# Four attention layers on one core: three output projections transposed, keys in chunks of 121, transposes of four heads in three banks, order by searched ranks

## The chip, the core and the metric

The kernel runs on one core of one Trainium2 chip. The time is device microseconds of one execution, and of several executions the median counts.

## What is computed

For each of 16 batches, `x` (100 queries by 256) passes through four cross-attention layers against one context (361 keys by 256), all in float32 with 16 heads. Each layer adds its output to a residual. L0 and L3 have heads of 16 columns, L1 and L2 of 64.

```
L0: q = LN(x) wq + bq; k, v = LN(ctx) wk + bk, wv + bv      # 16 heads of 16
    x = x + softmax(q k^T / 4) v wo + bo
    x = x + gelu(LN(x) w1 + b1) w2 + b2                      # 256 -> 1024 -> 256
L1: q = RMS(x) wq; k, v = ctx wk, ctx wv                     # 16 heads of 64
    x = x + softmax(q k^T) v wo                              # 1024 -> 256
L2: q, k = rope(x Wq), rope(ctx Wk); v = ctx Wv              # 16 heads of 64
    x = LN(x + softmax(mask(q k^T / 8)) v Wo) * gamma + beta # 1024 -> 256
L3: as L0's attention, with its own weights and norms
```

## The kernel before

**A plan, then an order.** Nothing is emitted while the layers are described. `plan.add` (L119) records each piece of work: the engines that may do it with an occupancy and a latency in ns, what it reads and writes, which buffer it takes, and for TensorE the tile shape (`mode`): `row64` and `row32` put several groups of contracted rows side by side, `col64` and `col32` several groups of output columns. `order` (L159) then walks through a list schedule: of the works whose inputs and buffers are at hand it takes the one that can start first, and among equals the one of lowest rank, `batch * 3e4 - tail`, where the tail is the longest chain behind it. A change of tile shape costs `MODE_SWITCH`, and 100 ns more if the present shape has run for under 1500 ns (L205 to L207). Copies out of PSUM may go to ACT or to VectorE, whichever the plan has ready first (`copied`, L542). The instructions are emitted in that order (L1206), and each engine runs its own in it.

**Batches.** Two batches are in flight: even ones use the buffers of parity 0, odd ones those of parity 1. SP loads context, x and mask two batches ahead; all 12 weight slabs stay in SBUF.

**Banks.** PSUM is a pool of 8 banks `ps` for everything; at most 4 hold scores.

**A unit of attention** (L726) is four heads. Their scores go into four banks, 100 queries by 361 keys each (L740). Per head: in L2 a minimum against the mask (L787), the negated row maximum on VectorE (L790), the exponential with its sum on ACT (L793); per pair of heads the reciprocal (L765); per head the division on POOL (L772). Then `transposed` (L805), once per pair: 12 transposes in `row64`, the two halves of the queries (64 and 36) into two banks, and two copies into a `pT` buffer, of which there are four, for two heads each. A chunk of keys is 128 columns (128, 128, 105), the last one padded with zeros. `weighted` (L835) multiplies by the values, accumulating over the three chunks, into one bank (L851), and copies it to `oT`, which holds the heads' outputs transposed: 128 columns of the concatenated heads by 100 queries, in two chunks (L0, L3) or eight.

**Projections.** Queries, keys and the hidden layer come out transposed (`project_T`, L632): weights stationary, activations moving. The output projection (`project_out`, L887) does it the other way round: a chunk of `oT` is stationary (100 columns), the weights move (256 columns), the result has the queries as rows, and VectorE adds the residual (L900). All these matmuls are issued at one line, L627 in `on_columns`. Where a layer needs its input transposed, `queries_T` (L593) makes it: four transposes and two copies. Norms are taken over rows of queries (`inv_root`, L553). `keys_T` (L643) transposes the context twice per batch, raw and normed, 12 transposes and three copies each. `add_row` (L877) adds a bias row to the residual on POOL.

Of the kernel before, what the change touches and what calls it, by code (L numbers as in the profile page):

```python
# [22 lines left out]
KC = (128, 128, SK - 256)  # L23
SKP = NKC * P
# [28 lines left out]

class Buf:
# [12 lines left out]
class Work:  # L67
    __slots__ = (
        "engines", "fn", "bufs", "takes", "next", "then", "n_after", "ready", "tail", "batch",
        "mode", "modes", "index", "start", "end", "engine",  # L70
# [4 lines left out]
HOP = 60  # L75
# [20 lines left out]
class Plan:  # L96

    MODE_SWITCH = {"row64": 160, "row32": 175, "col64": 145, "col32": 130, None: 190}

    KEEP_MODE, RUN = 100.0, 1500.0  # L100
# [4 lines left out]
    def __init__(self, slots):  # L105
        self.free = {c: [(0.0, i) for i in range(len(t))] for c, t in slots.items()}
        self.slots = slots
        self.work = []
        self.queue = {}
        self.turn = {}  # L110
        self.batch = 0

# [6 lines left out]
    def add(self, engines, fn, reads=(), writes=(), takes=(), mode=None, begun=()):  # L119
# [35 lines left out]
        w.ready = 0.0  # L155
        self.work.append(w)
        return w

    def order(self, lag):  # L159
# [4 lines left out]
        free_at = {e: 0.0 for e in ("PE", "ACT", "DVE", "POOL", "SP", "DMA")}  # L164
        mode, run = None, 0.0
        ready = [w for w in self.work if not w.n_after]
        left = len(self.work)
        turn = {c: 0 for c in self.queue}
        done = []
        while left:  # L170
            ready.sort(key=lambda w: w.batch * lag - w.tail)
            best = None
            held = set()
            for w in ready:
                t = w.ready
                ok = True
                need = {}
                for b in w.takes:
                    need[b.cls] = need.get(b.cls, 0) + 1
                for c, k in need.items():  # L180
                    if c in held:
                        ok = False
                        break
                    if c in self.queue:
                        mine = [b for b in w.takes if b.cls == c]
                        q = self.queue[c]
                        if q[turn[c] : turn[c] + k] != mine:
                            ok = False
                            break
                    slots = self.free[c]  # L190
                    if len(slots) < k:
                        ok = False
                        held.add(c)
                        break
                    t = max(t, sorted(slots)[k - 1][0])
                if not ok:
                    continue
                engine, cost = None, None
                for e, occ, lat in w.engines:
                    s = max(t, free_at[e])  # L200
                    if e == "PE" and mode not in w.modes:
                        lat = lat + self.MODE_SWITCH[w.modes[0]]
                    if cost is None or s + lat < cost - 1:
                        engine, cost, start = e, s + lat, s
                late = start  # L205
                if engine == "PE" and mode not in w.modes and run < self.RUN:
                    late += self.KEEP_MODE  # L207
                if best is None or late < best[0] - 1e-6:
                    best = (late, w, engine, cost, start)
            assert best is not None, [(w.index, [b.name for b in w.takes]) for w in ready[:20]]  # L210
            _, w, e, end, start = best
            occ = next(o for n, o, _ in w.engines if n == e)
            if e == "PE":
                run = run + occ if mode in w.modes else occ
                if mode not in w.modes:
                    mode = w.modes[0]
                    occ += self.MODE_SWITCH[mode]
                w.mode = mode
            free_at[e] = start + occ
            w.start, w.end, w.engine = start, end, e  # L220
            if e != "PE":
                w.mode = e
            for b in w.takes:
                slots = self.free[b.cls]
                slots.sort()
                _, i = slots.pop(0)
                b.slot, b.ap = i, self.slots[b.cls][i]
                if b.cls in turn:
                    turn[b.cls] += 1
            for b in w.bufs:  # L230
                b.left -= 1
                b.at = max(b.at, end + HOP)
                if not b.left and b.cls:
                    self.free[b.cls].append((b.at, b.slot))
            for x in w.next:
                x.n_after -= 1
                x.ready = max(x.ready, end + (0 if len(x.engines) == 1 and x.engines[0][0] == e else HOP))
                if not x.n_after:
                    ready.append(x)
            for x in w.then:  # L240
                x.n_after -= 1
                x.ready = max(x.ready, start)
                if not x.n_after:
                    ready.append(x)
            ready.remove(w)
            done.append(w)
            left -= 1
# [4 lines left out]
def tile_xattn_layers(  # L252
# [18 lines left out]
    def slots_of(name, n, shape, dtype=F32, pool=const):  # L271
# [8 lines left out]
        "pT": slots_of("pT", 4, [P, 2, NKC, S]),  # L280
# [11 lines left out]
    for p in range(2):  # L292
# [7 lines left out]
        slots[f"x{p}"] = slots_of(f"x{p}", 4, [S, E])  # L300
        slots[f"z{p}"] = slots_of(f"z{p}", 1, [S, E])
        slots[f"xT{p}"] = slots_of(f"xT{p}", 1, [P, 2, S])

# [5 lines left out]
    for t in slots["prob"]:  # L309
        nc.gpsimd.memset(t[:S, SK:], 0.0)  # L310
    for p in range(2):
# [13 lines left out]
    def load_inputs(b, issued=200.0, lands=4000.0):  # L325
# [3 lines left out]
        def issue(_):  # L329
            nc.sync.dma_start(  # L330
                out=ct.ap[:, 0:2, :], in_=ctx_kv[b, 0:256, :].rearrange("(c p) d -> p c d", p=P)
            )
            nc.sync.dma_start(out=ct.ap[: KC[2], 2, :], in_=ctx_kv[b, 256:SK, :])
# [219 lines left out]
    def inv_root(srcs, eps, name, square=False):  # L553
# [16 lines left out]
        def power(_):  # L570
# [5 lines left out]
            on_dve(350, k), stats, reads=[b for b, _, _ in srcs], writes=[mv]  # L576
# [16 lines left out]
    def queries_T(src, p, name):  # L593


        t = plan.buf(f"xT{p}", name)
# [7 lines left out]
        def fn(_):  # L604
# [7 lines left out]
            on_pe((64, 2), least=55), fn, reads=[src], writes=banks, takes=[t], mode="row64"  # L612
        )
        for i, (q0, q1) in enumerate(parts):
            copied(
                lambda q0=q0, q1=q1: t.ap[:, :, q0:q1], lambda i=i: tp(i), 2 * (q1 - q0),
                [banks[i]], [t],
            )
# [22 lines left out]
    HALVES = ((0, 64), (64, P))  # L641

    def keys_T(ct, cls, b):  # L643
# [4 lines left out]
        def tp(i):  # L648
            return banks[i].ap[:, : 2 * NKC * 64].rearrange("p (c j s) -> p c j s", c=2, j=NKC)

        def fn(_):
            for j, n in enumerate(KC):
                for c in range(2):
                    for i, (r0, r1) in enumerate(HALVES):
                        r1 = min(r1, n)
                        nc.tensor.transpose(
                            tp(i)[:, c, j, : r1 - r0], ct.ap[r0:r1, j, c * P : (c + 1) * P],
# [4 lines left out]
            on_pe((64, 2 * NKC), least=55), fn, reads=[ct], writes=banks, takes=[t], mode="row64"  # L662
        )

        def dst(i, j0, j1):
            a = t.ap[:, :, j0 * P : j1 * P].rearrange("p c (j s) -> p c j s", s=P)
            return a[:, :, :, 64 * i : 64 * i + 64]

        last = KC[2] - 64
        copied(lambda: dst(0, 0, NKC), lambda: tp(0), 2 * NKC * 64, [banks[0]], [t])  # L670
        copied(lambda: dst(1, 0, 2), lambda: tp(1)[:, :, 0:2, :], 4 * 64, [banks[1]], [t])
        copied(
            lambda: t.ap[:, :, 2 * P + 64 : SK], lambda: tp(1)[:, :, 2, :last], 2 * last,
            [banks[1]], [t],
        )
# [32 lines left out]
    class Attention:  # L708
# [17 lines left out]
        def unit(self, i):  # L726
# [27 lines left out]
            pTs = {}  # L754
            for u, pair in enumerate(pairs):
                pTs |= self.transposed([probs[h] for h in pair], pair, f"{name}_{i}_{u}")
# [48 lines left out]
        def transposed(self, probs, heads, name):  # L805

            banks = [plan.buf("ps", f"{name}_tp{t}") for t in range(2)]
            pT = plan.buf("pT", f"{name}_pT")
            parts = ((0, 64), (64, S))

            def tp(t):
                n = parts[t][1] - parts[t][0]
                return banks[t].ap[:, : 2 * NKC * n].rearrange("p (h c s) -> p h c s", h=2, c=NKC)

            def fn(_):
                for j, prob in enumerate(probs):
                    for c in range(NKC):
                        for t, (q0, q1) in enumerate(parts):
                            nc.tensor.transpose(  # L819
                                tp(t)[:, j, c, :], prob.ap[q0:q1, c * P : (c + 1) * P],  # L820
                                ident[q0:q1, q0:q1],
                            )

            plan.add(
                on_pe((64, 6), least=55), fn, reads=[*probs, self.v_buf(heads[0])], writes=banks,
                takes=[pT], mode="row64",
            )
            for t, (q0, q1) in enumerate(parts):
                copied(
                    lambda q0=q0, q1=q1: pT.ap[:, :, :, q0:q1], lambda t=t: tp(t),  # L830
                    2 * NKC * (q1 - q0), [banks[t]], [pT],
                )
            return {h: (pT, j) for j, h in enumerate(heads)}
# [74 lines left out]


    def small_heads_layer(L, b, xt, zT, names, fq, fk):  # L910
# [59 lines left out]
        for j, n in enumerate(KC):  # L970
            ps = plan.buf("ps", f"L{L}_v_ps_{b}_{j}")

            def values(mode, j=j, n=n, ps=ps):
                for c in range(2):
                    on_columns(
                        mode, lambda t0, t1: ps.ap[t0:t1, :E], zT.ap[:, c, j * P : j * P + n],
# [33 lines left out]
    def large_heads_layer(L, b, xt, xT, cT, names, rot, cap):  # L1010
# [48 lines left out]
        def values(half):  # L1059
            v = vb[half] = plan.buf(f"v{p}", f"L{L}_v_{b}_{half}")  # L1060
            for j, n in enumerate(KC):
                ps = plan.buf("ps", f"L{L}_v_ps_{b}_{half}_{j}")

                def fn(mode, j=j, n=n, ps=ps):
                    for c in range(2):
                        on_columns(
                            mode, lambda t0, t1: ps.ap[t0:t1, :], cT.ap[:, c, j * P : j * P + n],
# [28 lines left out]
        return project_out(att.oT, 8, wo, xt, p, f"L{L}_x_{b}")  # L1096

    def feed_forward(b, xt):
# [5 lines left out]
        resid = add_row(xt, f"ff_xb_{b}", "L0_xattn_b2", p, [rows_b])  # L1104
# [154 lines left out]
```

## Time and profile before

| | |
|---|---|
| median of 3 runs | 2068.08 us (2065.17 to 2068.21) |
| the profiled execution | 2067.87 us, its span 2066.0 us |
| TensorE clock granted | 0.988 of full speed over the span |
| instructions | 71,693, of which 29,665 matmul records and as many weight loads |
| costliest TensorE lines | L627 (all projections), L740 (scores), L851 (weighted sums), L819 (transposes of probabilities) |
| division on POOL (L772) | 1024 of 582 ns |
| exponential on ACT (L793) | 1024 of 567 ns, and 208 ns each to read the sum |
| maximum on VectorE (L790) | 1024 of 524 ns |
| copies to pT | 438 groups on ACT of 456 ns, 586 on VectorE of 418 ns |
| residual added on VectorE (L900) | 80 of 423 ns |
| from HBM / to HBM | 21.92 MB / 1.64 MB |

A float32 matmul leaves two matmul records, a transpose one. PE is TensorE's matmul side, PEld its weight loads, which overlap. A row of groups reads: line, engine, operation, what it writes and reads, rows*columns of the weights, moving operand, count, busy us, mean ns. A row of the timeline reads: start, length, group; the length of a group of matmuls runs to the end of its last one, which overlaps the next group, so costs are read from start to start. In brackets stands how long the engine was idle before it and what ended that.

### The profile page before, as it was taken

To read this page: it belongs to the slowest core of one execution; us is meant where nothing else is said; L and a number is where in the kernel's file an instruction comes from. 1 tells how busy PE (TensorE), PEld (TensorE's weight loads), DVE (VectorE), ACT (ScalarE), POOL (GpSimd) and SP (SyncE) were. 2 spreads that over 40 slices of the span, in tenths; PEclk is the share of its full clock that TensorE was granted. 3 is DMA by queue.
4 is the path that set the end of the run, shared out by engine and by line. 5 is a ranking of instruction groups with operands and counts; after the bars stand their busy time and mean duration, and the time that the engine had idled before them with its cause. 6 is when DMAs were issued, how large, how long until landed. Compare 5 with 4: busy or idle time off the path is not lost.

```text
span 2066.0 us, 71693 instructions
## 1 busy us (share of the span) xinstructions
PE 1993.2 (96%) x29665; PEld 1294.4 (63%) x29665; DVE 1375.9 (67%) x4058; ACT 1075.6 (52%) x3277; POOL 965.4 (47%) x1523
## 2 busy tenths in 40 slices
PE   8999999999999999999999999999999999999996
PEld 5666566575665656666575665756656566675664
DVE  5465666766677666766767667676776757667664
ACT  3445545555555455555555455554555545555453
POOL 4253545445354443644535354453545526455352
PEclk9999999999999999999999999999999999999996
DMA  7000000000000000000000000000000000000000
GB/s 285 2 2 12 4 10 4 4 12 5 12 5 3 11 5 12 5 11 4 5 12 4 12 3 4 12 4 12 5 2 12 4 12 4 10 5 4 2 4 3
DMA packets 14476, 28.13 MB, mean 14 GB/s; under 512 B 3346, under 2 KB 12360, under 8 KB 12616
## 3 DMA queue, kind: packets, MB, share of 16 engines
q1 hardware_dynamic: 14152, 23.56, 3.5%
q8 instruction: 233, 3.82, 0.8%
q14 instruction: 91, 0.75, 0.1%
HBM read 21.92 MB, written 1.64 MB: 11 GB/s over the span
## 4 chain that ended last, share of the span: by engine, by line
PE 85%; DVE 6%; POOL 4%; ACT 3%; issue 2%; DMA 0%; SPq 0%; DVEq 0%; ACTq 0%; POOLq 0%
PE ps L627 53%; PE ps L740 12%; PE ps L851 11%; PE ps L819 8%; ACT pT L547 3%; DVE two L790 1%; POOL prob L772 1%; POOL mv L571 1%; DVE ps L787 1%; DVE mv L561 1%; DVE ctxr L1145 1%; POOL kT L701 1%; PE ps L607 1%; PE ps L445 1%; DVE sw L689 1%
## 5 line engine op out<-in xcount | busy, mean ns | idle before, releaser
L772 POOL TENSOR_SCALAR prob<-prob,two 100x361 f32<-100x361 f32 x1024 | 578.2, 582 | 701.0 <-DVE two L765 544.4
L793 ACT ACTIVATE prob<-ps,two 100x361 f32<-100x361 f32 x1024 | 564.6, 567 | 149.2 <-DVE two L790 129.6
L790 DVE TENSOR_REDUCE two<-ps 100x1 f32<-100x361 f32 x1024 | 477.2, 524 | 193.3 <-PE ps L740 193.2
L627 PE MATMUL ps<-slab,cT 128*32 128x512 f32 (+3 forms) x2232 | 364.9, 596 | 3.7 <-ACT pT L547 3.7
L627 PE MATMUL ps<-cT,slab 128*64 128x361 f32 (+1 forms) x2360 | 351.0, 472 | 13.2 <-DVE kT L696 6.6
L547 ACT COPY pT<-ps 128x384 f32<-128x384 f32 (+1 forms) x438 | 185.7, 456 | 308.1 <-PE ps L819 220.1
L740 PE MATMUL ps<-kT,qT 32*100 32x181 f32 (+3 forms) x4096 | 301.5, 329 | 0.5 <-DVE qT L963 0.5
L819 PEld LDWEIGHTS ps<-ident,prob 64*128 64x128 f32 (+1 forms) x6144 | 227.4, 140 | 105.8 <-issue 58.7
L549 DVE COPY pT<-ps 128x216 f32<-128x216 f32 (+1 forms) x586 | 230.4, 418 | 93.4 <-PE ps L819 88.0
L740 PEld LDWEIGHTS ps<-kT,qT 32*100 32x100 f32 (+1 forms) x4096 | 227.5, 164 | 95.9 <-issue 39.9
L819 PE MATMUL ps<-ident,prob 64*128 64x64 f32 (+1 forms) x6144 | 261.9, 229 | 10.4 <-POOL prob L772 8.1
L627 PEld LDWEIGHTS ps<-cT,slab 128*64 128x64 f32 (+1 forms) x2360 | 132.6, 129 | 130.9 <-issue 95.4
L793 ACT ACTIVATION_READ_ACCUMULATOR prob<-ps,two 100x1 f32 x1024 | 212.6, 208 | 0.0
L627 PEld LDWEIGHTS ps<-slab,cT 128*32 128x32 f32 (+3 forms) x2232 | 94.8, 117 | 144.9 <-issue 134.1
L547 ACT COPY v<-ps 128x512 f32<-128x512 f32 (+1 forms) x151 | 88.7, 587 | 174.0 <-PE ps L627 174.0
L693 POOL TENSOR_TENSOR sw<-sw,rot 128x361 f32<-128x361 f32 x128 | 104.9, 822 | 157.0 <-DVE sw L689 148.1
L627 PE MATMUL ps<-xT,slab 128*64 128x100 f32 (+1 forms) x4576 | 172.6, 251 | 1.8 <-issue 1.4
L627 PEld LDWEIGHTS ps<-xT,slab 128*64 128x64 f32 (+1 forms) x4576 | 162.1, 126 | 19.3 <-issue 11.3
L851 PE MATMUL ps<-pT,v 128*64 128x100 f32 (+1 forms) x3072 | 157.1, 252 | 9.4 <-ACT pT L547 9.4
L851 PEld LDWEIGHTS ps<-pT,v 128*64 128x64 f32 (+1 forms) x3072 | 140.9, 137 | 35.1 <-issue 16.7
L627 PE MATMUL ps<-slab,oT 128*32 128x256 f32 (+2 forms) x1528 | 153.6, 386 | 0.0
L765 DVE RECIPROCAL two<-two 100x2 f32<-100x2 f32 x512 | 81.6, 160 | 91.3 <-ACT prob L793 86.2
(86 smaller groups left out, 1981.5 us busy)
## 6 DMA issues: line engine op xcount, KB each, us to landing
slab<-slabs_dram SPq DMA_DIRECT2D x12, 1024.0 KB
ctxr<-ctx_dram SPq DMA_DIRECT2D x16, 256.0 KB
ctxr<-ctx_dram SPq DMA_DIRECT2D x16, 105.0 KB
x<-x_dram SPq DMA_DIRECT2D x16, 100.0 KB
out_dram<-x SPq DMA_DIRECT2D x16, 100.0 KB
mask<-mask_dram SPq DMA_DIRECT2D x16, 45.1 KB
rows<-rowvecs_dram SPq DMA_DIRECT2D x1, 640.0 KB
cst<-consts_dram SPq DMA_DIRECT2D x1, 362.0 KB
```

Source lines behind the costliest of these rows:

```text
L445: nc.tensor.matmul(ps.ap[:, n : n + 1], lhsT=w[name][:, c, m * P : (m + 1) * P], rhs=col(b, c), start=(c == 0), stop=(c == 1),)
L547: nc.scalar.copy(dst(), src())
L549: nc.vector.tensor_copy(dst(), src())
L627: nc.tensor.matmul(out_f(t, t1), lhsT=lhsT[:, t:t1], rhs=rhs, start=start, stop=stop, tile_position=(0, t),)
L693: nc.gpsimd.tensor_tensor(a, a, wide(sin()), ALU.mult)
L740: nc.tensor.matmul(banks[h].ap[:S, k0:k1], lhsT=self.q_of(h), rhs=self.k_of(h)[:, k0:k1], start=(k0 == 0), stop=(k1 == SK), skip_group_che ...
L765: nc.vector.reciprocal(rsum.ap[:S], sums.ap[:S])
L772: nc.gpsimd.tensor_scalar(p.ap[:S, :SK], p.ap[:S, :SK], rsum.ap[:S, j : j + 1], 1.0, ALU.mult, ALU.mult,)
L790: nc.vector.tensor_reduce(neg_max.ap[:S, 0:1], s(), AX.X, ALU.max, negate=True)
L793: nc.scalar.activation(prob.ap[:S, :SK], s(), AF.Exp, bias=neg_max.ap[:S, 0:1], accum_out=sums.ap[:S, j : j + 1],)
L819: nc.tensor.transpose(tp(t)[:, j, c, :], prob.ap[q0:q1, c * P : (c + 1) * P], ident[q0:q1, q0:q1],)
L851: nc.tensor.matmul(ps.ap[t * w0 : (t + 1) * w0, cols], lhsT=lhsT, rhs=pTs[h][0].ap[:n, pTs[h][1], c, :], start=(c == 0), stop=(c == NKC - ...
```

## The change

1. **Projections transposed.** The output projections of the feed-forward, L1 and L2 use a new `project_out_T`: weights stationary (128 columns at a time, in column tiles of 64 or 32), `oT` moving (100 columns), the result transposed in a new buffer `rT` (two per parity), to which VectorE adds a residual that is transposed too. L0's and L3's keep the old form. After the feed-forward's `add_row` the residual is transposed once (`queries_T`, class `rT`). A new `rows_of` turns `rT` back into rows where a norm needs them: after the feed-forward and after L2. L2 takes L1's `rT` as its transposed input, and its own `queries_T` goes. `x` buffers: three per parity instead of four.
2. **Chunks of 121 keys** (121, 121, 119) instead of 128; padding to 363. `keys_T` cuts its halves at 64 and 121 and needs two copies instead of three. A memset on POOL at the start clears the last rows of the context's third chunk.
3. **Four heads in three banks.** `transposed` handles a unit's two pairs: the first 64 queries of each pair go into a bank of their own, the other 36 of all four heads into a third, shared one: three copies instead of four, into one `pT` buffer for four heads, of which there are two.
4. **The order.** The rank of a work gets a number by batch and one by its place in the batch, from a table; the costs of a change of tile shape, the reluctance to make one, and a pull to a shape with much work at hand are parameters too. The modelled hand-over is 75 ns instead of 60.

```diff
-KC = (128, 128, SK - 256)
-SKP = NKC * P
+KP = 121
+KC = (KP, KP, SK - 2 * KP)
+SKP = NKC * KP
...
+ORDER = {
+    "lag": 38400, "pull": 0.05, "window": 0,
+    "keep": {None: 890, "row64": 230, "row32": 260, "col64": 340, "col32": 1300},
+    "run": {None: 2660, "row64": 8610, "row32": 9590, "col64": 0, "col32": 580},
+    "batch": (-18000, 5000, 3000, 2500, 0, -3500, -2000, -500, 4000, 500, -500, -1500, -1500, 1500, 2000, -30500),
+    "place": [
+        100 * k for k in (
+        -449, 380, -410, -907, -297, -381, -841, -547, -865, -451, -58, -715, -384, -1275, -204,
...
-HOP = 60
+HOP = 75
...
-    MODE_SWITCH = {"row64": 160, "row32": 175, "col64": 145, "col32": 130, None: 190}
-
-    KEEP_MODE, RUN = 100.0, 1500.0
+    CHANGE = {"row64": 175, "row32": 204, "col64": 172, "col32": 160, None: 190}
...
+        for w in self.work:
+            w.rank = w.batch * ORDER["lag"] - w.tail
+            if w.batch >= 0:
+                w.rank = w.rank + ORDER["batch"][w.batch] + ORDER["place"][w.place]
...
-            ready.sort(key=lambda w: w.batch * lag - w.tail)
...
+            for c in able:
+                late = c[0]
+                if c[3] == "PE" and not c[5]:
+                    if run < ORDER["run"][mode]:
+                        late += ORDER["keep"][mode]
+                    late -= ORDER["pull"] * min(at_hand.get(c[2].modes[0], 0.0), 3000.0)
                 if best is None or late < best[0] - 1e-6:
-                    best = (late, w, engine, cost, start)
+                    best = (late, *c)
...
-        "pT": slots_of("pT", 4, [P, 2, NKC, S]),
+        "pT": slots_of("pT", 2, [P, 4, NKC, S]),
...
-        slots[f"x{p}"] = slots_of(f"x{p}", 4, [S, E])
+        slots[f"x{p}"] = slots_of(f"x{p}", 3, [S, E])
...
+        slots[f"rT{p}"] = slots_of(f"rT{p}", 2, [P, 2, S])
...
+    for t in slots["ctxr"]:
+        nc.gpsimd.memset(t[96:P, 2, :], 0.0)
...
+    def rows_of(src, p, name):
+
+        t = plan.buf(f"x{p}", name)
+        banks = [plan.buf("ps", f"{name}_ps{i}") for i in range(2)]
...
+        def fn(_):
+            for c in range(2):
+                for i in range(2):
+                    r = slice(64 * i, 64 * i + 64)
+                    nc.tensor.transpose(tp(i)[:, c, :], src.ap[r, c, :], ident[r, r])
...
-            for u, pair in enumerate(pairs):
-                pTs |= self.transposed([probs[h] for h in pair], pair, f"{name}_{i}_{u}")
+            pTs = self.transposed(probs, pairs, f"{name}_{i}")
...
+            rest = plan.buf("ps", f"{name}_tp_rest")
...
+            for u, pair in enumerate(pairs):
+                first = plan.buf("ps", f"{name}_tp{u}")
+
+                def fn(_, u=u, pair=pair, first=first):
+                    for j, h in enumerate(pair):
+                        for c in range(NKC):
+                            for (q0, q1), out in zip(
+                                parts, (tp(first, 2, 64)[:, j], tp(rest, 4, S - 64)[:, 2 * u + j])
+                            ):
+                                nc.tensor.transpose(
+                                    out[:, c, :], probs[h].ap[q0:q1, c * KP : (c + 1) * KP],
+                                    ident[q0:q1, q0:q1],
+                                )
...
+            copied(
+                lambda: pT.ap[:KP, :, :, 64:S], lambda: tp(rest, 4, S - 64), 4 * NKC * (S - 64),
+                [rest], [pT],
+            )
...
+    def project_out_T(oT, nch, wname, resid, p, name):
+
+        ps, t = plan.buf("ps", f"{name}_ps"), plan.buf(f"rT{p}", name)
+        wt = w[wname]
+
+        def fn(mode):
+            for m in range(2):
+                for c in range(nch):
+                    on_columns(
+                        mode, lambda t0, t1: ps.ap[t0:t1, m * S : (m + 1) * S],
+                        wt[:, c, m * P : (m + 1) * P], oT.ap[:, c, :], c == 0, c == nch - 1,
+                    )
+
+        def add(_):
+            nc.vector.tensor_tensor(
+                t.ap.rearrange("p c s -> p (c s)"), ps.ap[:, : 2 * S],
+                resid.ap.rearrange("p c s -> p (c s)"), ALU.add,
+            )
...
-        return project_out(att.oT, 8, wo, xt, p, f"L{L}_x_{b}")
+        return project_out_T(att.oT, 8, wo, resid, p, f"L{L}_x_{b}")
...
+        resid = queries_T(
+            add_row(xt, f"ff_xb_{b}", "L0_xattn_b2", p, [rows_b]), p, f"ff_r_{b}", "rT"
+        )
...
-        return project_out(hT, 8, "L0_xattn_w2", resid, p, f"ff_x_{b}")
+        return project_out_T(hT, 8, "L0_xattn_w2", resid, p, f"ff_x_{b}")
...
-        xt = feed_forward(b, xt)
+        resid = feed_forward(b, xt)
+        xt = rows_of(resid, p, f"ff_xt_{b}")
...
-        xt = large_heads_layer(1, b, xt, xT, cT, ("wq", "wk", "wv", "wo"), None, None)
-
-        xT = queries_T(xt, p, f"L2_xT_{b}")
+        resid = large_heads_layer(1, b, resid, xT, cT, ("wq", "wk", "wv", "wo"), None, None)
...
-        xt = large_heads_layer(2, b, xt, xT, cT, ("Wq", "Wk", "Wv", "Wo"), rot, cap)
+        resid = large_heads_layer(2, b, resid, resid, cT, ("Wq", "Wk", "Wv", "Wo"), rot, cap)
+        xt = rows_of(resid, p, f"L2_xt_{b}")
```

## The prediction

> **What bounds the kernel now.** I read the page first: engines, slices, and the chain that ended last.
>
> ```profile
> PE 1993.2 (96%) x29665; PEld 1294.4 (63%) x29665; DVE 1375.9 (67%) x4058; ACT 1075.6 (52%) x3277; POOL 965.4 (47%) x1523
> ...
> PE   8999999999999999999999999999999999999996
> ...
> PE 85%; DVE 6%; POOL 4%; ACT 3%; issue 2%; DMA 0%; SPq 0%; DVEq 0%; ACTq 0%; POOLq 0%
> ```
>
> TensorE is busy from the second slice to the last but one and carries 85% of the chain; no other engine passes 67%. So a stage is worth its TensorE time, and I count three things there: streaming, changes of tile shape, waits. The list of TensorE's waits, longest first, gives the third (total us, times, longest):
>
> ```profile
> PE ps L851 <- ACT pT L547: 17.3, 68, 1.3
> PE ps L627 <- ACT pT L547: 10.2, 46, 0.2
> PE ps L819 <- POOL prob L772: 8.1, 12, 1.6
> PE ps L627 <- DVE kT L696: 6.6, 13, 0.5
> ...
> PE ps L607 <- DVE z L583: 5.3, 1, 5.3
> ```
>
> The first two rows, 114 waits, are one pattern: a batch of transposes (L819), then at once a group that writes into the bank which the copy to pT is still emptying. The windows show where the rest is: 1600 to 2000 has 390.3 of 400 us busy, the last 66 us have 46.8, at a mean granted clock of 0.72.
>
> ```profile
> 1600.00:2000.00 400.00, 390.30 (x5978) 251.04 (x5970) 270.57 (x800) 210.01 (x639) 188.80 (x292) 1.00 0.02 6
> 2000.00:2066.00 66.00, 46.77 (x602) 34.27 (x598) 34.23 (x96) 25.18 (x81) 23.82 (x41) 0.72 0.01 3
> ```
>
> Prices come from the timeline of TensorE (start, length, group), from start to next start, since lengths overlap:
>
> ```profile
> 64.36 2.92 PE L627 MATMUL ps<-xT,slab 128*64 128x100 f32 x64
> 67.10 2.60 PE L627 MATMUL ps<-zT,slab 128*64 128x361 f32 x16
> ```
> ```profile
> 522.13 0.96 PE L819 MATMUL ps<-ident,prob 64*128 64x64 f32 x24
> 522.91 1.45 PE L740 MATMUL ps<-kT,qT 64*100 64x181 f32 x16
> ...
> 526.57 1.05 PE L627 MATMUL ps<-slab,oT 128*32 128x256 f32 x16
> 527.43 1.40 PE L627 MATMUL ps<-cT,slab 128*32 128x361 f32 x16
> ...
> 537.38 0.59 PE L819 MATMUL ps<-ident,prob 64*128 64x64 f32 x12
> 537.90 1.94 PE L627 MATMUL ps<-slab,cT 128*64 128x512 f32 x8
> ```
> ```profile
> 508.37 0.95 PE L819 MATMUL ps<-ident,prob 64*128 64x64 f32 x24
> 509.56 2.65 PE L627 MATMUL ps<-cT,slab 128*64 128x361 f32 x16 [0.24 <-ACT pT L547]
> ```
>
> **A. Three projections transposed: -33.6 us.** Old form: the row at 526.57 is two chunks of an output projection, 0.86 us; eight chunks 3.44 us. New form: 32 matmuls of 64 weight columns by 100 moving, two records each, which is exactly the x64 row at 64.36: 67.10 - 64.36 = 2.74 us. 0.70 us each, 3 per batch, 16 batches: 48 x 0.70 = 33.6 us, all on TensorE. (The weight slab becomes the stationary side, as in that row.)
>
> [...]
>
> **B. More transposes: +4.1 us.** Per batch the residual after the feed-forward is turned once (4) and rows are made back twice (8), and L2's own queries_T goes (4): +8, +128 in all. 24 of them take 0.78 us (522.13 to 522.91), 0.032 each. Their copies go to ACT and VectorE beside TensorE; the chain from the feed-forward to L1 and from L2 to L3 gets longer by a transpose and a copy, the one from L1 to L2 shorter. The other parity's batch covers that, except at the end (G).
>
> **C. Fewer changes of tile shape: -22.3 us.** In the two programs' instruction order successive matmuls change the shape 935 times before and 776 after. One change: 12 transposes are 0.38 us, and 537.38 to 537.90 is 0.52, so 0.14. 159 x 0.14 = 22.3. Other pairs of shapes cost from 0.05 to 0.17, so 8 to 27.
>
> **D. Chunks of 121: -9 us.** 6144 probability transposes load 121 weight columns instead of 128. By the single starts, a pair of transposes takes 62 ns whether the second moves 64 rows (L656) or 36 (L819), so the load limits it. No row shows 121; the groups of weight loads show two widths (count, busy us, mean ns):
>
> ```profile
> L819 PEld LDWEIGHTS ps<-ident,prob 64*128 64x128 f32 x3072 | 225.5, 140 | 105.4 <-issue 58.4 <-POOL prob L772 36.0 <-ACT prob L793 4.1
> ...
> L627 PEld LDWEIGHTS ps<-slab,oT 128*4 128x4 f32 x124 | 10.9, 88 | 0.0
> ```
>
> Lower end nothing; upper end 62 x 7/128 = 3.4 ns for 3072 pairs, 10.5 us. Only 52 of the 140 ns go with the columns: 7 of them are 2.9 ns, times 3072 = 9. I take that, the nearest row. The score, value and weighted matmuls keep their count and moved columns: nothing.
>
> **E. Waits behind transposes: -31 us.** 508.37 to 509.56 is 1.19 us; the same 24 transposes and a change are 0.75 + 0.14 = 0.89 when nothing waits. So a wait costs 0.30 us. Outside the last 60 us, the order before has 106 places where a bank is written again after at most 0.55 us of TensorE work since its last transpose; there the trace has 0.81 to 0.87 us from that transpose to the next write. The new order has 2 such places under 0.8 us and 16 under 0.9; most of the next ones have 1.04. 106 x 0.30 = 32, less some 1 that stays. Four heads' transposes also take three banks and three copies instead of four and four. The third copy waits for both pairs; behind it on ACT or VectorE stand exponentials and maxima of other units. Cover: at least 1.3 us of TensorE work lies between the last transpose and the weighted sum in 19 of 20 units.
>
> **F. Other waits: -3 us.** POOL prob and DVE kT waits outside the end come to some 11 us. From a score group's end to its transposes the new order has 6.1 us of TensorE work in L1 in its lowest twentieth (before 4.3) and 7.9 in L2 (before 6.5), in L0 and L3 4.8 (before 4.6): half of the 11 goes, 6. New: 29 times in mid-run the rows are transposed back 0.87 us of TensorE work after their projection, with a VectorE add between (0.42 us for 256 columns, now 200): up to 0.1 us each, 3. Ends: +6 and -11.
>
> **G. The end: -8 us.** From batch 15's last L2 projection (2023.70) to the end are 42 us, in which TensorE has 14.8 us of work at its usual rate; it waits 5.33 us for the first norm of L3 alone. In the new order 22.5 us of work follow that projection, because batch 14's L3 is drawn into it: 7.7 us move into waits. The chain gets one transpose and copy longer (1.2), and the low clock, which stands beside the idle time there, may last shorter. Ends: +2, if batch 14's exponentials (0.57 + 0.21 us each on ACT) delay batch 15's, and -15.
>
> **H. The start: +0.5 us.** The second context transfer, issued at 1.22 us, now waits for POOL's memset of that tile, which stands behind eight others (about 1.7 us). Behind it on SP's queue are x, colvecs, the first slab, consts and the mask; TensorE's first instruction waits for colvecs (6.3 us). SP's order is otherwise the same.
>
> Sum: -33.6 + 4.1 - 22.3 - 9 - 31 - 3 - 8 + 0.5 = -102.3. The profiled execution took 2067.87 us (its span 2066.0; median of the runs 2068.08): 2067.9 - 102.3 = 1965.6, **1966 us**.
>
> **Rivals.**
> 1. The new order shifts waits instead of removing them: its 0.2 us of margin at the bank reuses holds only if ACT and VectorE take the copy at once, and both are in order with instructions of 0.5 us. E, F and G at nothing: -60.3, 2008 us; half kept, 1987. For it: 230 us of copies on VectorE compete with maxima, masks and shuffles. Against: VectorE loses 300 of 884 copies and ACT gains 76 on 1041.
> 2. All waits in mid-run go and the end closes well: F -11, G -15, C at 27: another 20 us, 1946, down to 1935.
> 3. Slower: one pT slot now holds four heads and there are two. If weighted sums stood straight behind their third copy, each of 256 units would wait for a copy (0.46) and its two hand-overs (0.3): 0.76 x 256 = 195 us, 2160. It decides from 102/256 = 0.40 us a unit on. Against: only 5 of 256 units have under 1.0 us of TensorE work in that place.
> 4. The transposed projection gains nothing (A at nothing): 1999 us. Against: the x64 row has its very shape.
>
> **How the numbers follow.** Forecast, 1952 to 1982: 0.57. Rival 1: 0.24, most of it between 1982 and 2000. Rival 2: 0.11. Rival 3: 0.04. Rival 4: 0.03; 0.01 for no change. The range from 1937 to 2000 keeps the forecast, two thirds of rivals 1 and 4 and most of rival 2. 0.2%, some 4 us, is about what a measurement of this kernel can tell from no change. Faster 0.95, same 0.01, slower 0.04.
>
> **What would show it.** A: rows of x64 with rT or oT as moving side, 2.74 us to the next start. B: 30,809 matmul records. C: the changes of shape in the timeline. D: 24 transposes in 0.74 instead of 0.78 us. E: the two waits on ACT pT under 5 us together. F: POOL prob waits under 4. G: over 52 us busy in the last 66. It is wrong if the waits on copies (third copy, rows back) exceed 30 us, or if the clock falls below 0.98.

## The result and the profile after

The changed kernel takes **2081.76 us** (median of 4 runs, 2080.25 to 2082.37), against 2067.6 us for the kernel before in the same job: a ratio of **1.007, 95% interval 1.0052 to 1.0087**. It is slower, by some 14 us; the prediction of 1966 us, and its whole range, were wrong.

The page of the changed kernel, the lines that answer to the first ones of before:

```profile
span 2080.6 us, 72954 instructions
...
PE 2061.0 (99%) x30809; PEld 1438.2 (69%) x30809; DVE 1384.9 (67%) x3781; ACT 1127.1 (54%) x3330; POOL 954.4 (46%) x1524
...
PE   8999999999999999999999999999999999999998
...
PE 97%; DVE 1%; POOL 1%; issue 0%; DMA 0%; ACT 0%; SPq 0%; POOLq 0%; DVEq 0%; ACTq 0%
```

The first rows of its list of TensorE's waits:

```profile
PE ps L471 <- DMA crow<-colvecs_dram: 5.3, 1, 5.3
PE ps L503 <- DMA slab<-slabs_dram: 2.4, 1, 2.4
PE ps L936 <- DVE pT L607: 1.8, 3, 0.8
PE ps L665 <- DVE z L641: 1.4, 2, 1.0
PE ps L900 <- POOL prob L846: 1.2, 2, 0.8
PE ps L936 <- ACT pT L605: 1.1, 1, 1.1
```

Its windows, and the last 66 us (columns as before: stretch, PE busy, PEld, DVE, ACT, POOL, clock, DMA share, GB/s):

```profile
1200.00:1600.00 400.00, 400.00 (x6026) 278.44 (x6022) 274.48 (x752) 222.01 (x658) 188.41 (x299) 1.00 0.03 7
...
2014.00:2080.00 66.00, 57.97 (x852) 45.27 (x851) 40.47 (x111) 34.88 (x110) 24.58 (x44) 0.77 0.02 5
```

The waits that the prediction wanted gone are gone: TensorE is idle for 19.6 us in all (span less busy time; before 72.8), and for none of the 400 us from 1200 to 1600. Yet it is busy for 67.8 us more than before (2061.0 against 1993.2), where the terms A to D forecast 60.8 us less. So the loss is in the work itself. The timeline of TensorE (start, length, group) shows where:

```profile
521.46 1.48 PE L900 MATMUL ps<-ident,prob 64*121 64x64 f32 x24
522.75 1.45 PE L816 MATMUL ps<-kT,qT 64*100 64x181 f32 x16
524.04 1.38 PE L900 MATMUL ps<-ident,prob 64*121 64x64 f32 x24
525.35 0.72 PE L936 MATMUL ps<-pT,vs 121*32 121x100 f32 x24
```

From 521.46 to 522.75 are 1.29 us for 24 transposes of probabilities; before it was 0.78. The weight loads of the changed kernel by form (rows*columns of the weights; count, busy us, mean ns):

```profile
L900 PEld LDWEIGHTS ps<-ident,prob 64*121 64x121 f32 x3072 | 352.9, 185 | 76.5 <-issue 66.0 <-POOL prob L846 6.7 <-POOL qT L777 0.8
...
L691 PEld LDWEIGHTS ps<-ident,rT 64*100 64x100 f32 x128 | 6.2, 125 | 9.3 <-issue 7.5 <-DVE two L864 0.6 <-ACT prob L867 0.6
```

A load of 121 columns takes 185 ns, where one of 128 took 140. By the single starts (from the start of one matmul to that of the next but one), a pair of transposes takes 106 ns instead of 62: 44 ns for 3072 pairs are 135 us. The new transposes back into rows (L691), with 100 columns, take 125 ns and are not slow.

### The profile page after: what moved, and what is told of

It is laid out like the page before. It is cut to its first block, busy times and chain, and to the rows that moved or that the text cites. A ratio compares the mean times of both kernels' runs of the same rounds, so it can differ in the third digit from the quotient of the medians.

```text
span 2080.6 us, 72954 instructions
## 1 busy us (share of the span) xinstructions
PE 2061.0 (99%) x30809; PEld 1438.2 (69%) x30809; DVE 1384.9 (67%) x3781; ACT 1127.1 (54%) x3330; POOL 954.4 (46%) x1524
## 4 chain that ended last, share of the span: by engine, by line
PE 97%; DVE 1%; POOL 1%; issue 0%; DMA 0%; ACT 0%; SPq 0%; POOLq 0%; DVEq 0%; ACTq 0%
PE ps L709 55%; PE ps L900 17%; PE ps L816 13%; PE ps L936 11%; PE ps L665 1%; PE ps L738 1%; PE ps L503 1%; PE ps L691 0%; POOL prob L846 0%; DMA slab<-slabs_dram 0%; DVE two L864 0%; DVE pT L607 0%; POOL kT L777 0%; ACT prob L867 0%; PE ps L552 0%
## 5 line engine op out<-in xcount | busy, mean ns | idle before, releaser
L900 PEld LDWEIGHTS ps<-ident,prob 64*121 64x121 f32 (+1 forms) x6144 | 354.7, 185 | 76.5 <-issue 66.0
L900 PE MATMUL ps<-ident,prob 36*121 36x36 f32 (+1 forms) x6144 | 381.0, 272 | 1.3 <-POOL prob L846 1.2
L605 ACT COPY pT<-ps 121x384 f32<-121x384 f32 (+1 forms) x511 | 246.6, 490 | 248.9 <-PE ps L900 234.1
L709 PE MATMUL ps<-slab,cT 128*64 128x512 f32 (+2 forms) x2008 | 363.2, 596 | 0.0
L607 DVE COPY pT<-ps 121x432 f32<-121x432 f32 (+1 forms) x257 | 149.2, 582 | 147.9 <-PE ps L900 143.3
L709 PEld LDWEIGHTS ps<-slab,cT 128*64 128x64 f32 (+2 forms) x2008 | 92.8, 121 | 137.2 <-issue 122.5
L936 PEld LDWEIGHTS ps<-pT,v 121*64 121x64 f32 (+1 forms) x3072 | 138.7, 136 | 33.7 <-issue 21.5
L936 PE MATMUL ps<-pT,v 121*64 121x100 f32 (+1 forms) x3072 | 155.7, 251 | 0.0
L861 DVE TENSOR_TENSOR ps<-ps,cap 100x361 f32<-100x361 f32 x256 | 130.7, 533 | 21.4 <-PE ps L816 16.0
L605 ACT COPY v<-ps 121x512 f32<-121x512 f32 (+1 forms) x133 | 78.0, 586 | 114.7 <-PE ps L709 114.6
```

The source lines that it names most:

```text
L605: nc.scalar.copy(dst(), src())
L607: nc.vector.tensor_copy(dst(), src())
L709: nc.tensor.matmul(out_f(t, t1), lhsT=lhsT[:, t:t1], rhs=rhs, start=start, stop=stop, tile_position=(0, t),)
L861: nc.vector.tensor_tensor(s(), s(), self.cap.ap[:S, :], ALU.min)
L900: nc.tensor.transpose(out[:, c, :], probs[h].ap[q0:q1, c * KP : (c + 1) * KP], ident[q0:q1, q0:q1],)
L936: nc.tensor.matmul(ps.ap[t * w0 : (t + 1) * w0, cols], lhsT=lhsT, rhs=pTs[h][0].ap[:n, pTs[h][1], c, :], start=(c == 0), stop=(c == NKC - ...
```

## Experiments

The theory: an odd number of loaded columns costs a transpose the higher rate of its weight load, and everything else of the change gains what was forecast. The rivals: any number other than 128 does it; the odd distance of the rows, or the start of a chunk at an odd column, does it; or the other parts lose time too. The kernel before took 2068.01 us beside runs 1 to 4 and 2069.11 beside runs 5, 7, 8 and 9 (medians of 7), and 2069.68 (one run) beside run 6. `...` marks code left out.

**1. Chunks of 122 keys.** The buffer `two` is shortened for room; TensorE's order stays the same.

```
-KP = 121
+KP = 122
...
-        "two": slots_of("two", 40, [P, 2]),
+        "two": slots_of("two", 24, [P, 2]),
```

> The changed kernel with chunks of 122 keys instead of 121 (and fewer of the small two-column buffers, which leaves TensorE's order the same). Theory, weight loads of an odd number of columns run at half the rate: a pair of probability transposes takes 60 ns instead of 106, 3072 pairs save 141 us, about 1941 us. Rival, only a multiple of four is fast: pairs at 107 ns, about 2083 us. Rival, only 128 columns are fast: 107 ns, about 2083 us. Rival, the transposes are slow because of the three-bank form and not of their width: pairs stay at 106 ns in all four kernels, 2082 us.

Measured: 1973.43 us (1973.26 to 1975.03), ratio 0.9546 (0.953 to 0.9562). A pair of transposes takes 59 to 61 ns. One column more, and 108 us are gone; 122 is no multiple of four, so that isn't the condition. Expected were 141 us: TensorE's busy time does fall by 134.8 (2061.0 to 1926.2), but its idle time grows by 25.7 (19.6 to 45.3), which the expectation had left out. Its load:

```profile
L900 PEld LDWEIGHTS ps<-ident,prob 64*122 64x122 f32 x3072 | 211.4, 137 | 80.4 <-issue 35.1 <-POOL prob L846 33.4 <-POOL sw L769 5.8
```

**2. Chunks of 124** (`KP = 124`, `two` as in 1).

> Chunks of 124 keys, else as the kernel with 122. Theory (odd counts are slow): pair 61 ns, about 1944 us. Rival, a multiple of four is needed: also 61 ns, while 122 is slow. Rival, only 128 is fast: 109 ns, about 2088 us.

Measured: 1975.16 us (one run), pairs 60 to 61 ns, loads 137 ns. So 128 isn't the condition.

**3. Chunks of 127** (`KP = 127`, `two` as in 1; the buffer `wide` of the setup shares `sw`).

> Chunks of 127 keys (a start-up buffer shares another's space to make room). Theory (odd counts are slow): pair 112 ns, load 190 ns, about 2100 us. Rival, 121 is slow for another reason, for example too narrow a load: pair 62 ns, about 1950 us. Only 128 fast: 112 ns as well.

Measured: 2122.94 us (one run), pairs 111 ns. That is nearer to 128 than the two before, and slow:

```profile
L899 PEld LDWEIGHTS ps<-ident,prob 64*127 64x127 f32 x3072 | 368.2, 190 | 76.2 <-issue 59.5 <-POOL prob L845 7.6 <-POOL sw L768 5.8
```

It is 23 us above what was expected: its TensorE also starts 14 us late and its weight loads wait 6.8 us for the context's transfers, which is another thing (last section).

**4. Chunks of 128, all else as changed** (part 2 undone but for the memset and the two copies of `keys_T`; buffers as in 3).

```
-KP = 121
+KP = 128
...
-        "wide": slots_of("wide", 1, [P, 2, S]),
...
-        "two": slots_of("two", 40, [P, 2]),
+        "two": slots_of("two", 24, [P, 2]),
...
-                wide = plan.buf("wide", f"wide_{name}")
+                wide = plan.buf("sw", f"wide_{name}")
...
```

> Chunks of 128 keys as before, with the other three parts of the change. Theory (odd) and both width rivals: pair 62 ns as in the kernel before, 3072 x 44 ns = 135 us less than the changed kernel, about 1947 us, 0.94 of the kernel before. Rival, the three-bank form or the order is what costs: pairs at 106 ns, 2082 us.

Measured: **1971.97 us** (1971.03 to 1972.34), ratio 0.9535 (0.9521 to 0.955). The prediction without its term D is 2067.9 - 93.3 = 1974.6. So the other parts do together what was forecast, in part because two misses offset each other: busy time is 8.4 us lower than forecast, and 6.0 us less idle time goes (below). Its first waits, and the last 66 us of its windows:

```profile
PE ps L664 <- DVE z L640: 9.9, 15, 1.3
PE ps L690 <- DVE rT L1007: 7.0, 13, 0.5
PE ps L470 <- DMA crow<-colvecs_dram: 5.2, 1, 5.2
PE ps L502 <- DMA slab<-slabs_dram: 2.7, 1, 2.7
PE ps L899 <- POOL prob L845: 2.1, 3, 1.0
```
```profile
1904.00:1970.00 66.00, 55.77 (x934) 41.33 (x930) 46.75 (x130) 37.84 (x120) 31.62 (x55) 0.82 0.02 5
```

The difference between this kernel and the changed one, 2080.6 - 1970.3 = 110.3 us of span, is 128.0 us more busy time (2061.0 against 1933.0) less 17.7 us of waits (19.6 against 37.3): the slow transposes give VectorE time, and cover most of the first two rows above (16.9 us here, 1.4 there). These waits are what the expectation of 1947 us lacked.

**5. Chunks of 121, loads of 122.** Each transpose takes one column more than its chunk. That column lands in a row of `pT` that nothing reads, so nothing of the computation is left out or changed. The second chunk starts at the odd column 121.

```
-        "prob": slots_of("prob", 8, [P, SKP]),
+        "prob": slots_of("prob", 8, [P, SKP + 1]),
...
-                                    out[:, c, :], probs[h].ap[q0:q1, c * KP : (c + 1) * KP],
+                                    out[:, c, :], probs[h].ap[q0:q1, c * KP : (c + 1) * KP + 1],
...
```

> The changed kernel with its chunks of 121 keys, but each probability transpose loads 122 columns (one more than it needs; the extra row is used by nobody) and the probability buffers are 364 columns wide. The second chunk still starts at column 121, four bytes off an eight-byte boundary. Theory, the number of columns loaded must be even: pairs at 60 ns in all three chunks, about 1970 us. Rival, it is the start or the stride of 121 that is slow: pairs stay at 106 ns, 2082 us; or only the second chunk stays at 106 ns, about 2017 us.

Measured: **1965.69 us** (1962.88 to 1967.94), ratio 0.9504 (0.949 to 0.9518). It beats both kernels. Timeline and loads:

```profile
493.25 0.92 PE L900 MATMUL ps<-ident,prob 64*122 64x64 f32 x24
493.99 1.45 PE L816 MATMUL ps<-kT,qT 64*100 64x181 f32 x16
```
```profile
L900 PEld LDWEIGHTS ps<-ident,prob 64*122 64x122 f32 x3072 | 209.6, 136 | 80.2 <-issue 35.3 <-POOL prob L846 33.0 <-POOL sw L769 5.8
```

24 transposes are 0.74 us, and a pair takes 59 to 60 ns in each of the three chunks, the one at the odd start too. So neither chunks of 121 nor an odd start is slow.

**6. Rows 364 apart, loads of 121.** Run 5 altered the distance of the rows and the count together; this one only the distance.

```
-        "prob": slots_of("prob", 8, [P, SKP]),
+        "prob": slots_of("prob", 8, [P, SKP + 1]),
```

> The changed kernel with one thing altered: the rows of prob lie 364 values apart instead of 363; each transpose still loads 121 columns. Theory (an odd count of loaded columns halves the load's rate, wherever the rows lie): pairs of transposes stay at 106 ns, loads at 185 ns, about 2082 us. Rival (the odd distance of the rows does it; the run with 122 columns changed the distance and the count together): pairs 60 ns, loads 136 ns, about 1966 us.

Measured: 2079.98 us (one run), pairs 106 ns:

```profile
L900 PEld LDWEIGHTS ps<-ident,prob 64*121 64x121 f32 x3072 | 353.0, 185 | 76.3 <-issue 65.9 <-POOL prob L846 6.7 <-POOL qT L777 0.8
```

With 121 columns the distance does nothing, and between this run and run 5, at one distance, the count decides. The three rivals on the load are out. An odd distance with an even count wasn't run.

The next three ask what the parts are worth without the searched order. All three were expected too low.

**7. Chunks of 128 in the old order**: run 4 with part 4 undone (the old ranks and costs, those of transposes and norms in the plan too).

```
-    "lag": 38400, "pull": 0.05, "window": 0,
+    "lag": 30000, "pull": 0.0, "window": 0,
...
+    "batch": (0,) * 16,
+    "place": (0,) * 1000,
...
-HOP = 75
+HOP = 60
```

> The kernel with chunks of 128 keys and the ranks, the reluctance and the costs of the order set back to those of the kernel before (batch times 30000 less the tail, 100 ns, 1500 ns; only part 4 undone). Its order has 950 changes of tile shape instead of 776. Theory, the order removes the shape changes and most of the waits: 174 x 0.14 = 24 us and some 35 us of waits come back, about 2031 us. Rival, the three banks alone removed the waits: only the 24 us come back, about 1996 us.

Measured: 2192.92 us (2173.43 to 2197.72), ratio 1.0586 (1.0537 to 1.0634), granted clock 0.945. Its first waits, and two of its windows:

```profile
PE ps L860 <- POOL prob L806: 34.3, 28, 1.9
PE ps L625 <- DVE z L601: 32.9, 15, 5.3
PE ps L896 <- ACT pT L565: 10.7, 18, 1.0
```
```profile
520.00:560.00 40.00, 38.27 (x662) 25.64 (x660) 27.08 (x73) 23.83 (x70) 15.12 (x25) 1.00 0.01 2
560.00:600.00 40.00, 35.52 (x448) 27.44 (x450) 20.14 (x60) 16.09 (x52) 14.81 (x25) 0.83 0.06 15
```

Against the kernel before, idle time rises from 72.8 to 136.8 us, and busy time from 1993.2 to 2055.5. By terms A and B, and 15 changes of tile shape more (950 against 935, 0.14 us each), busy time should have fallen by 27.4; so 90 us of it have another cause. The clock fell from 0.988 to 0.945, an estimate of 2055.5 x (1 - 0.945/0.988) = 89 us. I had priced neither the new waits nor the clock.

In the second row, 14 waits of 1.97 us are for L3's norm, after L2's rows are turned back: this is the longer chain of step B. And the lower clock stands behind such waits. A wait of TensorE, and the window right after it (clock in the third column from the end):

```profile
579.62 0.34 PE L625 MATMUL ps<-ident,z 64*128 64x64 f32 x4 [1.97 <-DVE z L601]
```
```profile
579.90:586.70 6.80, 6.32 (x52) 5.06 (x52) 3.88 (x12) 2.91 (x11) 2.22 (x4) 0.50 0.08 19
```

Away from its first and last 70 us the trace has 34 stretches at half clock, of 3.4 or 6.8 us, 191 us in all (an estimate: 96 us of clock lost). In the 8 us before each, waits of TensorE sum to 1.4 to 3.4 us. In runs 4 and 5 and in the changed kernel no wait there is longer than 0.8 us, and no such stretch begins.

**8. Part 1 alone in the old order**: the kernel before with `project_out_T`, `rows_of`, the `rT` buffers and three `x` buffers.

```
+        slots[f"rT{p}"] = slots_of(f"rT{p}", 2, [P, 2, S])
...
-        return project_out(att.oT, 8, wo, xt, p, f"L{L}_x_{b}")
+        return project_out_T(att.oT, 8, wo, resid, p, f"L{L}_x_{b}")
```

> The kernel before with the three transposed projections alone (part 1). Its order has 1054 changes of tile shape instead of 935. Theory: -33.6 for the projections, +4.1 for the transposes, 119 x 0.14 = +17 for the changes, waits as before: about 2055 us. Rival, the transposed form gains nothing: 2089 us. Rival, the row count hides behind waits: below 2040 us.

Measured: 2111.21 us (2109.93 to 2113.0), ratio 1.0211 (1.0194 to 1.0228). Busy time is 1994.7 us, as before, at a granted clock of 0.979 (an estimate: 1994.7 x (1 - 0.979/0.988) = 18 us lost by it). Idle time is 113.4 instead of 72.8, and the new part is in one row (before: 5.3, once):

```profile
PE ps L607 <- DVE z L583: 51.0, 27, 5.3
```

Two kinds of wait are in it:

```profile
703.52 0.34 PE L607 MATMUL ps<-ident,z 64*128 64x64 f32 x4 [0.74 <-DVE z L583]
...
757.22 0.44 PE L607 MATMUL ps<-ident,z 64*128 64x64 f32 x4 [2.66 <-DVE z L583]
```

Twelve of 0.74 us, 8.9 us in all, are for L3's norm, after L2's rows are turned back: the longer chain of step B. But 14 of 2.0 to 2.9 us, 36.9 us in all, are for L0's norm of a new batch's `x`, which hangs on no projection; it stands on VectorE among the norm of that batch's context, and TensorE has nothing else at hand. So most of the new idle time isn't the chain's, but comes with the order that the plan makes by the old ranks. There are also 1054 changes of shape, 119 more than before.

**9. Part 2 alone in the old order** (the kernel before with chunks of 121).

```
-KC = (128, 128, SK - 256)
-SKP = NKC * P
+KP = 121
+KC = (KP, KP, SK - 2 * KP)
+SKP = NKC * KP
```

> The kernel before with chunks of 121 keys alone (part 2). Theory: 3072 pairs of transposes at 106 instead of 62 ns, 135 us, less the waits for POOL that this covers (some 5): about 2198 us. Rival, the slow loads hide in the waits behind the transposes: 2198 less 35, about 2163 us.

Measured: 2240.33 us (one run), granted clock 0.972; expected was 2198. Busy time grows by 160.8 us (2154.0), idle time by 11.7. The 135 us of the loads are there; the lower clock can account for the rest, 26 us of busy time (an estimate: 2154.0 x (1 - 0.972/0.988) = 35).

## Why the prediction was wrong, point by point

**The step that failed is D.** "No row shows 121 ... Lower end nothing; upper end 62 x 7/128" took the 128 columns of the old transposes as the nearest row and let fewer columns cost less, and gave the term no bound on the losing side. It was forecast at -9; between run 4 and the changed kernel part 2 is worth +110 us, with even loads (run 5) some -6. Two rows of the same view of weight loads, which the prediction didn't show, should have warned:

```profile
L740 PEld LDWEIGHTS ps<-kT,qT 64*100 64x100 f32 x2048 | 152.1, 164 | 30.9 <-issue 16.4 <-ACT prob L793 4.5 <-ACT qT L547 2.7
...
L627 PEld LDWEIGHTS ps<-slab,oT 128*36 128x36 f32 x516 | 56.9, 114 | 21.2 <-issue 0.3
```

A load of 100 columns took longer (164 ns) than the transposes' load of 128 (140). With the 88 ns at 4 columns, the ordinary loads go up by (164 - 88) / 96 = 0.79 ns a column, the 128 of a transpose by (140 - 88) / 124 = 0.42. So, by this estimate, the transposes already loaded at about twice the rate of the ordinary loads, and a shape without a row of its own could fall back to the ordinary one: 88 + 117 x 0.79 = 181 ns at 121 columns, 41 more for each of 3072 pairs, 126 us. That was the upper bound to give. Measured were 185 ns a load and 44 ns more a pair. Neither of the two signs by which the prediction was to be wrong came (the waits on copies in the changed kernel are 2.9 us, the clock 0.988); only its line on D did, 1.29 us for 24 transposes instead of 0.74.

From 121 to 127 columns the odd loads go from 185 to 190 ns, 0.83 ns a column, near the 0.79 of the ordinary ones. So the runs show these float32 transposes loading fast with 100, 122, 124 and 128 columns (125 to 140 ns) and slowly with 121 and 127. What makes a load fast, no run shows.

The other steps, read in run 4, where D is absent. **A to C** were forecast at -51.8 together; busy time fell by 60.2 (1993.2 to 1933.0). A's price holds: an x64 row with `oT` moving takes 2.75 us there to the next start (2.74 forecast). The old form was priced from two chunks in tiles of 32; its eight-chunk rows, in tiles of 64, stood in the trace of before too (the first two rows below: 3.55 us; 3.44 was put), so the agreement was partly luck. Over 47 such rows each the mean to the next start is 3.58 us before and 2.80 in run 4, changes of shape included: 0.77 x 48 = 37 us, 33.6 forecast.

```profile
541.37 3.62 PE L627 MATMUL ps<-slab,qT 128*64 128x256 f32 x32
544.92 1.48 PE L740 MATMUL ps<-kT,qT 64*100 64x181 f32 x16
...
299.79 2.92 PE L708 MATMUL ps<-oT,slab 128*64 128x100 f32 x64
302.54 1.38 PE L708 MATMUL ps<-cT,slab 128*64 128x361 f32 x8
```

What part 1 is worth by itself in the new order, waits included, wasn't run. B's 30,809 records are there. **E** is right in the main: the two rows of waits behind transposes, 27.5 us, come to 1.1 (2.9 with the copies on VectorE), some 25 us of the 31 forecast. **F** missed: the waits on POOL prob went from 8.1 to 2.1 and those on DVE kT from 6.6 to nothing, more than the 6 us put, but the rows turned back wait 0.54 us, 13 times, not up to 0.1: 7.0 us where 3 were put. And 8.7 us of run 4's first row are 14 waits of 0.62 us for L0's norm of a new batch's `x`, behind VectorE's norm of the context, as in run 8; the prediction has no term for them. **G** is right: 55.77 of the last 66 us are busy (over 52 was forecast; before 46.77). **E to H** were forecast at -41.5; idle time fell by 35.5 (72.8 to 37.3). **H** has no weight: TensorE starts at 5.2 us in run 4 and at 5.3 in the changed kernel, not at 6.3 plus 0.5, and by 6.0 and 6.3 in runs 6 and 5, which issue the same transfers as the changed kernel, a start varies by 1 us.

The rivals: none had a load that gets slower. Rival 3's mechanism (each unit waiting for its `pT` copy) did not occur; waits on `pT` sum to 2.9 us in the changed kernel. Rival 1 asked the right thing of the order in the wrong direction: in the old order part 1 loses 42 us, parts 1 and 3 lose 124; in the new one the same kernel is 96 us faster than before. Whether an order searched for the kernel before would have gained as much wasn't run, so how the 96 us split between the order and the parts is open. And the slow transposes hid themselves from the list of waits, which had never looked better.

## What to carry to other kernels

Before a shape is changed, put the rows of that operation and of its neighbours side by side by size: where a larger one is faster than a smaller one (here 140 ns for 128 columns, 164 for 100), a new size must be priced at both rates. A smaller operand may cost more (185 ns for 121 columns), and the range must allow for it. And a change of the work is to be tried with an order made for it: parts 1 and 3 lost 124 us in the old order, and with the new one the kernel gained 96. A row of waits is to be taken apart by place first: run 8's one row held two kinds, and the larger wasn't the one that the change suggests.

## What the runs showed of the hardware that was not expected

**Odd counts.** Transposes of the float32 probabilities with 121 and 127 loaded columns: loads of 185 and 190 ns, pairs of 106 and 111. With 122, 124 and 128: 136 to 141 ns, pairs of 59 to 62. Those back into rows, with 100: 125 ns. An odd start made no difference (run 5: 59 to 60 ns a pair in all three chunks), nor, with 121, a distance of the rows of 363 or 364 (run 6: 106 ns a pair at both). Ordinary loads with odd counts aren't slower: 25 and 57 columns take 103 and 131 ns in the changed kernel, where 88 + 0.79 ns a column beyond 4 gives 105 and 130 (an estimate). Why is open.

**The rows of a transfer.** With 127 rows a chunk the context's first transfers hold SP up. Its issues in run 3:

```profile
0.72 0.32 SPq L386 DMA_DIRECT2D ctxr<-ctx_dram  x1
2.06 6.19 SPq L390 DMA_DIRECT2D ctxr<-ctx_dram  x1
8.29 4.67 SPq L391 DMA_DIRECT2D x<-x_dram  x1
```

The second and third take 6.19 and 4.67 us there, 0.29 and 0.31 in the changed kernel. TensorE's first instruction comes at 19.7 us in run 3, at 11.8 with 124 rows, at 10.7 with 122, at 5.2 with 128 and at 5.3 in the changed kernel with 121. The mean busy share of the 16 DMA engines in the first 4 us is 0.04 with 127, 0.13 with 124, 0.15 with 122, 0.34 with 128 and 0.39 with 121. Neither follows the number of rows. The context's last rows are a transfer of their own, 107, 113, 117, 105 and 119 rows. What sets the share, no run shows. Run 5, with chunks of 121, has 0.39 too and starts at 6.3 us, so run 1, at 10.7, loses some 4 us there.

**The clock.** In run 7 the granted clock falls to 0.83 and 0.87 in single stretches of 40 us in mid-run, where no wait between 400 and 1600 us is longer than 2.0 us. Cut finer, the clock there is full or half, and the half follows waits: one of 1.97 us, or several that sum to 1.4 us or more within 8 us. Not every such wait is followed by one: run 7 has one of 1.98 us, run 8 four of 2.7, without. The half-clock stretches last 3.4 or 6.8 us, and in run 7 no single wait as long stands before them; shorter ones do. What else decides, no run shows.
